# Gamma folded into the first attention's weights, x1 made on GpSimd, fewer steps in a row in the first batch's last norm, and all of y ahead of the first experts

## The chip, the cores and the metric

The kernel runs on one core of one Trainium2 chip. A core has five engines with queues of their own: TensorE (PE; its weight loads are shown apart as PEld), VectorE (DVE), ScalarE (ACT), GpSimd (POOL) and SyncE (SP, which here only issues DMAs). The metric is the device time of one execution in microseconds; lower is better. Each queue is worked off in order, and an instruction at its head that waits for another engine holds up all behind it.

## What is computed

The reference, cut to what matters (8 batches of 512 tokens with 128 channels, all float32):

```python
xn  = layernorm(layernorm(x)) * gamma + beta       # inside the attention
qkv = xn @ w_qkv; q, k, v = heads of 4 x 32
q = q * 32 ** -0.5;  k = softmax(k, over the tokens)
context = k^T v per head;  out = (q context) @ w_out + b_out
attn = out + layernorm(x)
x = x + layernorm(attn)
h = layernorm(x)
ffn = sum over 8 experts of (silu(h @ Wg) * (h @ Wu)) @ Wd     # 128 -> 512 -> 128
x = x + layernorm(ffn)
```

The attention is a linear one: for each batch it comes down to one 128 x 128 matrix (context, masked to the four heads, times w_out), by which q is multiplied. The code calls that matrix `m`, the normed input plus the output bias `x1b`, and the attention's output with the residual `y`.

## The kernel before, in words

**Stages.** A batch is held as four tiles of 128 tokens (`NJ` = 4). Batch 0 goes through `opening()`, which is tuned for latency, since nothing else can run yet; the attention of every later batch is spread over the expert steps of the batches before it. The experts of one batch are 32 steps (8 experts by 4 column blocks of 128); one step is a matmul into `g` (L1080), one into `u` (L1081), a Silu on ACT (L1085) and a product on DVE (L1105). For a batch of 512 tokens the second expert matrix is then applied in `down_pairs` (L935).

**Batch 0.** Its first 16 steps are cut by tokens, so that they can begin before all tokens are ready. The list `units` (L868 to L871) has: steps 0 and 1 for tile 0, steps 0 and 1 for tile 1, steps 2 to 15 for tiles 0 and 1 together, steps 0 to 15 for tiles 2 and 3, and then steps 16 to 31 for all four.

**The order** of every queue is the order of the program text (`manual_schedule`): there is no scheduler. Generators (`prepare`, `first_pieces`, `after_m`) are advanced by `next(...)` where their instructions are to stand, and `plan()` gives for each step the calls that are put behind that step's product.

**The opening**, in order of what needs what:

- The statistics of x (`both_stats`, L189): per tile a bn_stats and a bn_aggr on DVE, then `scale(h)` and a power of -1/2 on GpSimd (L212) for the double norm. A layernorm of a layernorm is computed in one go from mean and variance.
- `norm_apply` (L260) makes `xh`; PE transposes it (L429, L363); ACT and DVE bring it out of PSUM while they apply gamma and beta (L430, L436, L443), which gives `xnT`.
- `keys` (L374): PE product, DVE maximum (L379), ACT Exp (L380). `values`, `turn_keys`, `context`, `query` and `masked` follow; L467 and L468 put `m` together from the two halves of the tokens, whose softmax sums were taken apart.
- `first_norm` (L366) makes x1 on DVE and adds the bias on GpSimd (L372). Tiles 0 and 1 are made in the opening, tiles 2 and 3 in the steps of tile 1 (L971).
- `first_pieces` (L675) handles tiles 0 and 1: PE adds x1b (by a product with the identity) and q m into `y` (L684, L687); then come DVE statistics (L696 to L700), the power for `rstd` on GpSimd (L701), a covariance of x and y (L706), from which the variance of the sum x + norm(y) follows without another pass, a second power (L713), the normed input `z` of the experts (L719), its transpose (L725) and the copy to `zT` (L726), for which the first expert matmul waits.
- `after_m` (L752) does the same for tiles 2 and 3, in pieces behind steps 4 to 13 of the unit of tiles 0 and 1 (L977, L978): y on PE (L762, L765) behind step 4, statistics behind 5, covariance behind 6 and 7, GpSimd's part (L785 to L787) behind 8, norm and residual (L789, L790) behind 9, `z` (L792, which is L260 in the profile) behind 11, and its transpose on PE (L794, L269 in the profile) behind 12.
- `prepare` makes, beside the opening, what the later batches need of the weights: `wqT`, `gwv` and the constant part `mb` of m. `keep_warm` (L161) lets PE do products that nobody reads.

**Weights.** SP issues 24 loads of 256 KB for the experts, one after another, while the opening runs. `weight_sums` (L887) and `differences` (L895 to L897) are elementwise work on GpSimd for the later products.

Of the kernel before, what the change touches and what calls it, by code (L numbers as in the profile page):

```python
# [16 lines left out]
def kernel(  # L17
# [45 lines left out]
    P = 128  # L63
# [75 lines left out]
    gwv = const.tile([P, C], F32, name="gwv")  # L139
    mb = const.tile([P, C], F32, name="mb")  # L140

    def prepare():


        t = ps_acc.tile([P, N], F32, tag="accB", name="w_ps")
        nc.tensor.transpose(t[:, :C], w_qkv_sb[:, 0:C], ident)
        nc.scalar.mul(gwv, w_qkv_sb[:, 2 * C : 3 * C], gamma_sb)
        nc.scalar.mul(wqT, t[:, :C], QSCALE)
        yield
        nc.tensor.matmul(t[:, :1], w_qkv_sb[:, 2 * C : 3 * C], beta_sb, start=True, stop=True)  # L150
        bv = const.tile([P, 1], F32, name="bv")
        nc.scalar.copy(bv, t[:, :1])
        bvw = work.tile([P, C], F32, tag="gs", name="bvw")
        nc.scalar.mul(bvw, w_out_sb, bv)
        yield
        nc.tensor.matmul(t[:, :C], heads, bvw, start=True, stop=True)
        yield
        nc.scalar.copy(mb, t[:, :C])
        yield

    def keep_warm(moving, count=1):  # L161

        t = ps_acc.tile([P, N], F32, tag="accA", name="unread")
        for i in range(count):
            nc.tensor.matmul(
                t[:, : moving.shape[1]], moving[:, :P], moving,
                start=(i == 0), stop=(i == count - 1),
            )
# [20 lines left out]
    def both_stats(src):  # L189

        stats = const.tile([P, NJ, 6], F32, name="stats_0")
        mv = [const.tile([P, 2, 2], F32, name=f"mv_0_{h}") for h in range(2)]
        ve = [const.tile([P, 4], F32, name=f"ve_0_{h}") for h in range(2)]
        rstd = [const.tile([P, 4], F32, name=f"rstd_0_{h}") for h in range(2)]

        def one(j):
            nc.vector.bn_stats(stats[:, j, :], src[:, j])  # L200

        def aggregate(j):
            nc.vector.bn_aggr(mv[j // 2][:, j % 2, :], stats[:, j, :])

        def add(h):
            nc.vector.tensor_scalar_add(ve[h][:, :2], mv[h][:, :, 1], EPS)

        def scale(h):
            nc.vector.scalar_tensor_tensor(
                ve[h][:, 2:], ve[h][:, :2], EPS, mv[h][:, :, 1], ALU.mult, ALU.add  # L210
            )
            nc.gpsimd.tensor_tensor(rstd[h][:, 2:], ve[h][:, 2:], mhalf[:, :2], ALU.pow)  # L212

        for call, i in (
            (one, 0), (one, 1), (one, 2), (aggregate, 0), (aggregate, 1), (one, 3), (add, 0),
            (aggregate, 2), (scale, 0), (aggregate, 3), (add, 1), (scale, 1),
        ):
            call(i)
        return [(mv[h], rstd[h][:, :2], rstd[h][:, 2:], ve[h]) for h in range(2)]
# [91 lines left out]
    def opening():  # L311
# [12 lines left out]
        xnT = work.tile([P, N], F32, tag="xnT", name="xnT_0")  # L324
# [29 lines left out]
        weights = prepare()  # L354
        next(weights)
        keep_warm(w_qkv_sb[:, :W])
# [9 lines left out]
        def first_norm(j):  # L366
            h, i = divmod(j, 2)
            nc.vector.tensor_scalar(
                x1[:, j], xt[:, j], s1[h][0][:, i, 0:1], s1[h][1][:, i : i + 1],
                ALU.subtract, ALU.mult,  # L370
            )
            nc.gpsimd.tensor_tensor(x1b[:, j, :], x1[:, j, :], bias_sb, ALU.add)  # L372

        def keys(h):  # L374
            k_ps.append(bank(f"k_ps{h}", "ps" if h else "u"))
            nc.tensor.matmul(
                k_ps[h][:, :W], w_qkv_sb[:, C : 2 * C], xnT[:, COL[h]], start=True, stop=True
            )
            nc.vector.tensor_reduce(kmax[:, h : h + 1], k_ps[h][:, :W], AX.X, ALU.max, negate=True)  # L379
            nc.scalar.activation(  # L380
                ekT[:, COL[h]], k_ps[h][:, :W], AF.Exp, bias=kmax[:, h : h + 1],
                accum_out=ksum[:, h : h + 1],
            )

        def values(h):
            v_ps.append(bank(f"v_ps{h}", "u" if h else "g"))
            for j in H:
                nc.tensor.matmul(
                    v_ps[h][:, j * C : (j + 1) * C],
                    xnT[:, (2 * h + j) * P : (2 * h + j + 1) * P], w_qkv_sb[:, 2 * C : 3 * C],  # L390
                    start=True, stop=True,
                )

        def turn_keys(h):
# [5 lines left out]
            return t[:, :W]  # L400
# [10 lines left out]
        def query(lo, hi, tag, at=0):  # L411
            if not at:
                q_ps.append(bank(f"q_ps{lo}", tag))
            t = q_ps[-1][:, at : at + (hi - lo) * P]
            r = slice(lo * P, hi * P)
            nc.tensor.matmul(t, w_qkv_sb[:, 0:C], xnT[:, r], start=True, stop=True)
            nc.scalar.mul(qT[:, r], t, QSCALE)
# [10 lines left out]
        for j in H:  # L428
            nc.tensor.transpose(t[:, j * P : (j + 1) * P], xh[:, j, :], ident)  # L429
        nc.scalar.activation(  # L430
            xnT[:, COL[0]], t[:, :W], AF.Identity, bias=beta_sb, scale=gamma_sb
        )
        next(weights)
        norm_apply(xh[:, J[1]], xt[:, J[1]], (s1[1][0], s1[1][2]))
        t = [turn(j, "g") for j in (2, 3)]
        nc.scalar.activation(  # L436
            xnT[:, 2 * P : 3 * P], t[0], AF.Identity, bias=beta_sb, scale=gamma_sb
        )
        next(weights)
        for h in H:  # L440
            nc.gpsimd.tensor_tensor(s1[h][1], s1[h][3][:, :2], mhalf[:, :2], ALU.pow)
        first_norm(0)
        nc.vector.tensor_scalar(xnT[:, 3 * P :], t[1], gamma_sb, beta_sb, ALU.mult, ALU.add)  # L443
        keys(0)
        keys(1)
        values(0)
        values(1)
        t0, t1 = turn_keys(0), turn_keys(1)
        nc.vector.tensor_tensor(kmax[:, 2:3], kmax[:, 0:1], kmax[:, 1:2], ALU.min)

        nc.scalar.activation(part, kmax[:, :2], AF.Exp, bias=kmax[:, 2:3], scale=-1.0)
        for h in H:
            nc.vector.tensor_copy(v[:, COL[h]], v_ps[h][:, :W])
        nc.vector.tensor_copy(ek[:, COL[0]], t0)
        nc.scalar.copy(ek[:, COL[1]], t1)
        query(0, 1, "u")
        context(0)
        context(1)
        query(1, 2, "g")
        nc.vector.tensor_tensor(ksum[:, 2:4], ksum[:, 0:2], part, ALU.mult)  # L460
        nc.vector.tensor_tensor(ksum[:, 2:3], ksum[:, 2:3], ksum[:, 3:4], ALU.add)
        first_norm(1)
        nc.vector.reciprocal(rsum, ksum[:, 2:3])
        masked(0)
        nc.vector.tensor_scalar(part, part, rsum, None, ALU.mult)
        masked(1)
        nc.vector.tensor_scalar(m, m_ps[0][:, :C], part[:, 0:1], None, ALU.mult)  # L467
        nc.vector.scalar_tensor_tensor(m, m_ps[1][:, :C], part[:, 1:2], m, ALU.mult, ALU.add)  # L468
# [4 lines left out]
        keep_warm(flat(xt[:, J[0]]), 2)  # L473
        next(first)
        keep_warm(yn[:, 0], 2)
        next(first)
        rest.extend((first, second, first_norm))
# [197 lines left out]
    def first_pieces(xt, s1, qT, m, x1b, x2, yn, z, zT):  # L675

        mvx, vex = s1[0][0], s1[0][3]
# [3 lines left out]
            for p, t in ((ps, "ps"), (ps_acc, "accB"))  # L681
# [11 lines left out]
        stats, mv, ve, rstd = tile_("pst", 6), tile_("pmv", 2), tile_("pve"), tile_("prs")  # L693
        cov, rv, t, rstd2 = tile_("pco"), tile_("prv"), tile_("pt"), tile_("prt")
        for j in R:
            nc.vector.bn_stats(stats[j], y[j])  # L696
        for j in R:
            nc.vector.bn_aggr(mv[j], stats[j])
        for j in R:
            nc.vector.tensor_scalar_add(ve[j], mv[j][:, 1:2], EPS)  # L700
            nc.gpsimd.tensor_tensor(rstd[j], ve[j], mhalf[:, :1], ALU.pow)  # L701

        nm = const.tile([P, 1], F32, name="pnm_0")

        def covariance(j):
# [3 lines left out]
            nc.scalar.mul(cov[j], cov[j], 2.0 / C)  # L709
# [5 lines left out]
        def residual(j):  # L715
            nc.vector.tensor_tensor(x2[:, j], yn[:, j], xt[:, j], ALU.add)

        def last(j):
            nc.vector.tensor_scalar(  # L719
                z[:, j], x2[:, j], mvx[:, j, 0:1], rstd2[j], ALU.subtract, ALU.mult  # L720
            )

        def turn(j):
            t_ps = ps.tile([P, N], F32, tag="ps", name=f"z_ps_0{j}")
            nc.tensor.transpose(t_ps[:, :P], z[:, j], ident)  # L725
            (nc.vector.tensor_copy if j else nc.scalar.copy)(  # L726
                zT[:, j], t_ps[:, :P].rearrange("c (a i) -> c a i", a=NQ)
            )

        for j in R:  # L730
            nc.vector.reciprocal(rv[j], ve[j])
            nc.scalar.activation(
                rv[j], rv[j], AF.Identity, bias=vex[:, j : j + 1], scale=mv[j][:, 1:2]
            )
        covariance(0)
        nc.vector.tensor_scalar(yn[:, 0], y[0], mv[0][:, 0:1], rstd[0], ALU.subtract, ALU.mult)
        scale(0)
        covariance(1)
        nc.vector.scalar_tensor_tensor(nm, mv[1][:, 0:1], -1.0, rstd[1], ALU.mult, ALU.mult)
        nc.scalar.activation(yn[:, 1], y[1], AF.Identity, bias=nm, scale=rstd[1])  # L740
        residual(0)
        scale(1)
        yield
        last(0)
        turn(0)
        residual(1)
        last(1)
        yield
        turn(1)
        yield  # L750
# [192 lines left out]
    def plan(b, lo, hi, begin):  # L943
# [24 lines left out]
        if hi - lo == 1:  # L968
            if lo:
                for i in range(2):  # L970
                    at(i, lambda i=i: rest[2](2 + i))  # L971
            else:
                p["first"] = lambda: next(rest[0])
        elif b == 0 and begin < FIRST:
            if not lo:
                go = lambda: next(rest[1], None)
                at(4, go, go)  # L977
                for i in (5, 6, 7, 8, 9, 11, 12, 13):  # L978
# [178 lines left out]
```

## Time and profile before

| quantity | value |
|---|---|
| median of 3 runs | 687.84 us (687.75 to 688.28) |
| the profiled execution | 687.67 us |
| its span in the trace | 685.7 us |
| granted TensorE clock, mean | 0.999 |
| PE busy | 678.5 us, 99% of the span |
| DVE, ACT, POOL busy | 301.6, 248.5, 428.2 us |
| share of PE in the chain that ended last | 98% |
| first expert matmul starts at | 17.33 us |
| second half's transpose (L269) starts at | 30.20 us |

The span is the time from the first to the last recorded instruction; the profiled execution is 2.0 us longer than it. The chain that ended last is found from the last instruction backwards, at each step to what released it. A timeline row gives the start, the duration, the engine, the line and the operation with its tiles, and in brackets how long the engine had been idle and what ended that.

### The profile page before, as it was taken

The numbers are of one execution on the slowest core, as the hardware profiler recorded it, in microseconds if no ns is written. First come the engines' busy times: TensorE is split into PE (matmuls) and PEld (weight loads), VectorE is DVE, ScalarE is ACT, GpSimd is POOL, SyncE is SP. The second block draws the span as 40 slices with busy tenths as digits, with TensorE's granted clock in tenths as the row PEclk, the third lists the DMA queues.
The fourth block names the chain that finished last, engine by engine and source line by source line (L and its number), as shares of the span: only waits on it lengthen the run. The fifth ranks groups of instructions, "written<-read, shape, count | busy, mean of one in ns | idle before, by whom it ended". The sixth has DMA issues, their size and how long they took to land.

```text
span 685.7 us, 9319 instructions
## 1 busy us (share of the span) xinstructions
PE 678.5 (99%) x3187; PEld 376.8 (55%) x3187; DVE 301.6 (44%) x806; ACT 248.5 (36%) x486; POOL 428.2 (62%) x535
## 2 busy tenths in 40 slices
PE   8999999999999999999999999999999999999997
PEld 6875565445654455544654446544465445644576
DVE  6656404555055541554324642356513545043425
ACT  5464422454125451254413443145412442033212
POOL 4399895584747656475755749557494583767501
PEclk9999999999999999999999999999999999999999
DMA  8511022010020210101111101100012000010020
GB/s 264 170 32 48 15 61 78 0 61 30 20 77 1 61 32 32 62 21 41 32 46 48 32 31 33 67 26 32 31 33 77 1 31 1 17 62 0 1 78 16
DMA packets 36671, 30.82 MB, mean 45 GB/s; under 512 B 3984, under 2 KB 28048, under 8 KB 36624
## 3 DMA queue, kind: packets, MB, share of 16 engines
q1 hardware_dynamic: 36336, 30.03, 13.7%
q8 instruction: 25, 0.41, 0.3%
q14 instruction: 22, 0.18, 0.1%
q10 hardware_dynamic: 288, 0.20, 0.1%
HBM read 18.42 MB, written 11.80 MB: 44 GB/s over the span
## 4 chain that ended last, share of the span: by engine, by line
PE 98%; DVE 1%; DMA 0%; POOL 0%; issue 0%; ACT 0%; POOLq 0%; DVEq 0%
PE g L1080 32%; PE u L1081 32%; PE accA L935 16%; PE accB L935 12%; PE g_ps L483 1%; PE y_ps L579 1%; PE k_ps L547 1%; PE end L822 1%; DMA x<-in_L_attn_x_dram 0%; PE end_A L822 0%; PE end_B L822 0%; PE c_ps L492 0%; PE wa_ps L504 0%; PE m_ps L498 0%; PE c_ps L406 0%
## 5 line engine op out<-in xcount | busy, mean ns | idle before, releaser
L1105 DVE TENSOR_TENSOR h<-sg,u 128x512 f32<-128x512 f32 (+2 forms) x266 | 172.5, 650 | 336.2 <-PE u L1081 311.3
L1085 ACT ACTIVATE sg<-g 128x512 f32<-128x512 f32 (+2 forms) x282 | 156.4, 556 | 362.4 <-PE g L1080 341.0
L1080 PE MATMUL g<-zT,wg 128*128 128x512 f32 (+2 forms) x564 | 267.0, 555 | 0.4 <-ACT zT L726 0.4
L1081 PE MATMUL u<-zT,wu 128*128 128x512 f32 (+2 forms) x564 | 265.8, 553 | 0.0
L895 POOL TENSOR_TENSOR t<-h 128x512 f32<-128x512 f32 x124 | 157.9, 1274 | 123.4 <-PE accB L935 62.9
L1081 PEld LDWEIGHTS u<-zT,wu 128*128 128x128 f32 x564 | 106.9, 190 | 113.3 <-issue 109.3
L1080 PEld LDWEIGHTS g<-zT,wg 128*128 128x128 f32 x564 | 102.3, 190 | 96.1 <-issue 92.0
L935 PE MATMUL accA<-h,wd 128*64 128x256 f32 x620 | 145.7, 380 | 0.0
L935 PE MATMUL accB<-t,ws 128*64 128x256 f32 x496 | 137.8, 380 | 0.0
L935 PEld LDWEIGHTS accA<-h,wd 128*64 128x64 f32 x620 | 84.3, 137 | 40.7 <-PE u L1081 3.8
L897 POOL TENSOR_TENSOR h<-h,t 128x256 f32<-128x256 f32 x124 | 90.6, 730 | 9.7
L896 POOL TENSOR_TENSOR t<-h,t 128x256 f32<-128x256 f32 x124 | 90.2, 727 | 9.7
L935 PE MATMUL accA<-t,ws 128*64 128x256 f32 x248 | 73.8, 379 | 0.0
L935 PE MATMUL accB<-h,ws 128*64 128x256 f32 x248 | 73.8, 379 | 0.0
L245 POOL TENSOR_TENSOR rstd<-ve,mhalf 128x4 f32<-128x4 f32 (+1 forms) x28 | 32.8, 1170 | 60.3 <-DVE nm L243 49.1
L935 PEld LDWEIGHTS accB<-t,ws 128*64 128x64 f32 x496 | 67.3, 137 | 0.0
L935 PEld LDWEIGHTS accB<-h,ws 128*64 128x64 f32 x248 | 34.0, 137 | 17.9
L935 PE MATMUL accB<-h,wd 128*64 128x256 f32 x124 | 36.9, 379 | 0.0
L935 PEld LDWEIGHTS accA<-t,ws 128*64 128x64 f32 x248 | 34.0, 137 | 0.0
L253 ACT ACTIVATE fn<-q,nm,rstd 128x128 f32<-128x128 f32 x28 | 11.5, 482 | 39.2 <-POOL nm L246 39.2
L253 ACT ACTIVATE x<-x,nm,rstd 128x128 f32<-128x128 f32 x56 | 22.9, 482 | 3.1 <-POOL nm L246 2.4
L186 POOL TENSOR_TENSOR rstd<-ve,mhalf 128x2 f32<-128x2 f32 (+1 forms) x4 | 2.5, 632 | 31.3 <-DVE ve L184 31.2
(202 smaller groups left out, 403.8 us busy)
## 6 DMA issues: line engine op xcount, KB each, us to landing
wg<-in_L_ffn_Wg_dram SPq DMA_DIRECT2D x8, 256.0 KB, 6.0
wu<-in_L_ffn_Wu_dram SPq DMA_DIRECT2D x8, 256.0 KB, 5.9
wd<-in_L_ffn_Wd_dram SPq DMA_DIRECT2D x8, 256.0 KB, 6.1
bounce<-f_blkA SPq DMA_DIRECT2D x8, 256.0 KB, 2.0
fA<-bounce SPq DMA_DIRECT2D x32, 64.0 KB, 2.0
bounce<-f_blkB SPq DMA_DIRECT2D x8, 256.0 KB, 2.1
fB<-bounce SPq DMA_DIRECT2D x32, 64.0 KB, 2.0
x<-in_L_attn_x_dram SPq DMA_DIRECT2D x7, 256.0 KB, 2.7
```

The source lines that it names most:

```text
L245: nc.gpsimd.tensor_tensor(rstd, ve, mhalf[:, :n], ALU.pow)
L253: nc.scalar.activation(d, t, AF.Identity, bias=nm[:, i : i + 1], scale=rstd[:, i : i + 1])
L483: nc.tensor.matmul(g_ps[:, :C], xh[:, j, :], ek[:, :, j * Q : (j + 1) * Q], start=(j == 0), stop=(j == NJ - 1),)
L547: nc.tensor.matmul(k_ps, w_qkv_sb[:, C : 2 * C], self.xnT, start=True, stop=True)
L895: nc.gpsimd.tensor_tensor(t[:, 0:2], h[:, 1::2], h[:, 0:2], ALU.subtract)
L896: nc.gpsimd.tensor_tensor(t[:, 2], h[:, 3], t[:, 0], ALU.subtract)
L897: nc.gpsimd.tensor_tensor(h[:, 1], h[:, 2], t[:, 2], ALU.subtract)
L935: nc.tensor.matmul(o, w, r, start=start, stop=stop)
L1080: nc.tensor.matmul(g_ps[:, :cols], wg_sb[e][:, w], zT, start=True, stop=True)
L1081: nc.tensor.matmul(u_ps[:, :cols], wu_sb[e][:, w], zT, start=True, stop=True)
L1085: nc.scalar.activation(sg[:, :cols], g_ps[:, :cols], AF.Silu)
L1105: nc.vector.tensor_tensor(flat(h2)[:, first : first + cols], sg[:, :cols], u_ps[:, :cols], ALU.mult)
```

## The change

Five things are changed, all in the work of batch 0 up to its first 16 steps.

1. **Gamma goes into the weights.** `prepare` multiplies the key and value weights by gamma on ACT (`gwk`, `gwv`), DVE does the query weights (`gwq`). What comes out of the transposes is only copied (`xhT`). Beta drops out of the keys (a softmax over tokens does not see a constant), enters the queries as a bias `bq`, and the values through `mb`, which is added when `m` is made. `prepare` thus has two products with beta in place of one, and its later pieces stand further back.
2. **GpSimd makes x1** of all four tiles in the opening, with a tensor_scalar in place of DVE's; the bias addition stays there.
3. **The last norm of tiles 0 and 1 has fewer steps in a row.** The scaling of the covariance is folded into constants, `x2` is first left without its means, the mean that belongs to it is one [P, 1] value, and GpSimd puts x2 right later, in place.
4. **All of y precedes the first experts**: the two first pieces of `after_m` are called in the opening, and its other pieces move ahead by one or two steps; the transpose from step 12 to step 11.
5. Order: the statistics of tiles 0 and 1 are aggregated before those of tile 2 begin; both maxima precede the Exps; copies stand in `values` and `turn_keys`, the second ones on ACT; all queries stand behind the contexts; the unread products are fewer and go to another PSUM buffer.

The diff, cut to its core:

```diff
-    def prepare():
+    def prepare(s1):
         t = ps_acc.tile([P, N], F32, tag="accB", name="w_ps")
-        nc.tensor.transpose(t[:, :C], w_qkv_sb[:, 0:C], ident)
+        nc.tensor.transpose(t[:, C : 2 * C], w_qkv_sb[:, 0:C], ident)
+        nc.scalar.mul(gwk, w_qkv_sb[:, C : 2 * C], gamma_sb)
         nc.scalar.mul(gwv, w_qkv_sb[:, 2 * C : 3 * C], gamma_sb)
-        nc.scalar.mul(wqT, t[:, :C], QSCALE)
-        yield
-        nc.tensor.matmul(t[:, :1], w_qkv_sb[:, 2 * C : 3 * C], beta_sb, start=True, stop=True)
-        bv = const.tile([P, 1], F32, name="bv")
-        nc.scalar.copy(bv, t[:, :1])
+        yield
+        for k, i in enumerate((2, 0)):
+            nc.tensor.matmul(
+                t[:, k : k + 1], w_qkv_sb[:, i * C : (i + 1) * C], beta_sb, start=True, stop=True
+            )
+        b = const.tile([P, 2], F32, name="b_vq")
+        nc.scalar.copy(b, t[:, :2])
+        yield
...
         nc.scalar.copy(mb, t[:, :C])
+        nc.scalar.mul(wqT, t[:, C : 2 * C], QSCALE)
+        nc.scalar.mul(bq, b[:, 1:2], QSCALE)
         yield
...
         def scale(h):
-            nc.vector.scalar_tensor_tensor(
-                ve[h][:, 2:], ve[h][:, :2], EPS, mv[h][:, :, 1], ALU.mult, ALU.add
+            nc.vector.tensor_scalar(
+                ve[h][:, 2:], mv[h][:, :, 1], 1 + EPS, EPS * EPS, ALU.mult, ALU.add
             )
             nc.gpsimd.tensor_tensor(rstd[h][:, 2:], ve[h][:, 2:], mhalf[:, :2], ALU.pow)
 
         for call, i in (
-            (one, 0), (one, 1), (one, 2), (aggregate, 0), (aggregate, 1), (one, 3), (add, 0),
-            (aggregate, 2), (scale, 0), (aggregate, 3), (add, 1), (scale, 1),
+            (one, 0), (one, 1), (aggregate, 0), (aggregate, 1), (one, 2), (scale, 0), (one, 3),
+            (aggregate, 2), (aggregate, 3), (add, 0), (scale, 1), (add, 1),
         ):
...
         def first_norm(j):
-            nc.vector.tensor_scalar(
+            nc.gpsimd.tensor_scalar(
                 x1[:, j], xt[:, j], s1[h][0][:, i, 0:1], s1[h][1][:, i : i + 1],
                 ALU.subtract, ALU.mult,
             )
             nc.gpsimd.tensor_tensor(x1b[:, j, :], x1[:, j, :], bias_sb, ALU.add)
...
-        nc.scalar.activation(
-            xnT[:, COL[0]], t[:, :W], AF.Identity, bias=beta_sb, scale=gamma_sb
-        )
-        next(weights)
+        nc.scalar.copy(xhT[:, COL[0]], t[:, :W])
         norm_apply(xh[:, J[1]], xt[:, J[1]], (s1[1][0], s1[1][2]))
         t = [turn(j, "g") for j in (2, 3)]
-        nc.scalar.activation(
-            xnT[:, 2 * P : 3 * P], t[0], AF.Identity, bias=beta_sb, scale=gamma_sb
-        )
-        next(weights)
+        nc.scalar.copy(xhT[:, 2 * P : 3 * P], t[0])
         for h in H:
             nc.gpsimd.tensor_tensor(s1[h][1], s1[h][3][:, :2], mhalf[:, :2], ALU.pow)
-        first_norm(0)
-        nc.vector.tensor_scalar(xnT[:, 3 * P :], t[1], gamma_sb, beta_sb, ALU.mult, ALU.add)
+        for j in range(NJ):
+            first_norm(j)
+        nc.vector.tensor_scalar(gwq, w_qkv_sb[:, 0:C], gamma_sb, None, ALU.mult)
+        nc.vector.tensor_copy(xhT[:, 3 * P :], t[1])
+        nc.vector.tensor_scalar(vx, s1[0][3][:, :2], 1.0, C / 2, ALU.add, ALU.mult)
+        next(weights)
         keys(0)
         keys(1)
+        softmax(0)
+        softmax(1)
         values(0)
         values(1)
-        t0, t1 = turn_keys(0), turn_keys(1)
         nc.vector.tensor_tensor(kmax[:, 2:3], kmax[:, 0:1], kmax[:, 1:2], ALU.min)
+        turn_keys(0)
+        turn_keys(1)
         nc.scalar.activation(part, kmax[:, :2], AF.Exp, bias=kmax[:, 2:3], scale=-1.0)
-        for h in H:
-            nc.vector.tensor_copy(v[:, COL[h]], v_ps[h][:, :W])
-        nc.vector.tensor_copy(ek[:, COL[0]], t0)
-        nc.scalar.copy(ek[:, COL[1]], t1)
-        query(0, 1, "u")
+        next(weights)
         context(0)
         context(1)
+        next(weights)
+        query(0, 1, "u")
         query(1, 2, "g")
+        masked(0)
         nc.vector.tensor_tensor(ksum[:, 2:4], ksum[:, 0:2], part, ALU.mult)
         nc.vector.tensor_tensor(ksum[:, 2:3], ksum[:, 2:3], ksum[:, 3:4], ALU.add)
-        first_norm(1)
         nc.vector.reciprocal(rsum, ksum[:, 2:3])
-        masked(0)
+        masked(1)
         nc.vector.tensor_scalar(part, part, rsum, None, ALU.mult)
-        masked(1)
...
         next(first)
         query(2, 4, "u")
-        keep_warm(flat(xt[:, J[0]]), 2)
+        next(second)
         next(first)
-        keep_warm(yn[:, 0], 2)
+        next(second)
+        keep_warm(flat(xt[:, J[0]]), 1)
         next(first)
...
+        def residual(j):
+            nc.vector.scalar_tensor_tensor(
+                x2[:, j], y[j], rstd[j], xt[:, j], ALU.mult, ALU.add
+            )
+            nc.vector.scalar_tensor_tensor(
+                mean[j], mv[j][:, 0:1], rstd[j], mvx[:, j, 0:1], ALU.mult, ALU.add
+            )
+        def last(j):
+            nc.vector.tensor_scalar(
+                z[:, j], x2[:, j], mean[j], rstd2[j], ALU.subtract, ALU.mult
+            )
...
+        inverse(0)
         covariance(0)
-        nc.vector.tensor_scalar(yn[:, 0], y[0], mv[0][:, 0:1], rstd[0], ALU.subtract, ALU.mult)
+        inverse(1)
         scale(0)
+        residual(0)
         covariance(1)
-        nc.vector.scalar_tensor_tensor(nm, mv[1][:, 0:1], -1.0, rstd[1], ALU.mult, ALU.mult)
-        nc.scalar.activation(yn[:, 1], y[1], AF.Identity, bias=nm, scale=rstd[1])
-        residual(0)
-        scale(1)
         yield
         last(0)
         turn(0)
+        scale(1)
         residual(1)
         last(1)
         yield
         turn(1)
+        for j in R:
+            nc.gpsimd.tensor_scalar(
+                x2[:, j], x2[:, j], mean[j], mvx[:, j, 0:1], ALU.subtract, ALU.add
+            )
         yield
...
                 go = lambda: next(rest[1], None)
-                at(4, go, go)
-                for i in (5, 6, 7, 8, 9, 11, 12, 13):
+                for i in (3, 4, 5, 6, 7, 9, 11):
                     at(i, go)
```

In the new order ACT makes both `zT` copies (with a factor) ahead of the first Silu, and GpSimd's queue has: two powers, two powers, four pairs of tensor_scalar and addition for x1, the two powers of `rstd`, the two last powers, the two corrections of x2, then the second half's work and the weight sums.

## The prediction

> **What bounds the kernel.** I read the page's busy times and its chain first. PE is busy 99% of the span, and the chain that ended last is 98% PE:
>
> ```profile
> PE 678.5 (99%) x3187; PEld 376.8 (55%) x3187; DVE 301.6 (44%) x806; ACT 248.5 (36%) x486; POOL 428.2 (62%) x535
> ...
> PE 98%; DVE 1%; DMA 0%; POOL 0%; issue 0%; ACT 0%; POOLq 0%; DVEq 0%
> ```
>
> From 31 us on, PE's groups show 0.0 us idle. So whatever is won or lost before that moves the end by the same amount, and only three places can change: the start of the experts, products that PE does not have to fit in between them, and PE's waits among the first steps. The chain in order of time shows all three:
>
> ```profile
> 13.03 0.47 PE y_ps_ps L687 x2
> ...
> 14.40 0.57 POOL prs L701
> ...
> 15.65 0.56 POOL prt L713
> ...
> 17.33 0.49 PE g L1080 x2
> ...
> 22.29 0.44 PE y_ps L762 x4
> 22.73 0.45 PE y_ps L765 x4
> ...
> 29.75 0.85 DVE z L260 x2
> 30.60 0.04 issue
> 30.65 0.33 PE z_ps L269
> ```
>
> Up to 17.33 us the path is one latency after another over DVE, ACT, GpSimd and PE. At 22.29 the second half's y takes 0.44 + 0.45 us out of the experts' stream. At 29.75 PE waits for the second half's z.
>
> **Products moved (a sure gain).** y of tiles 2 and 3 goes from behind step 4 into the opening: 0.44 + 0.45 = 0.89 us less in PE's stream. In the opening it stands behind the queries. There PE only does unread products (13.99 to 15.02 and 15.55 to 16.2 us in the timeline) and idles. It needs qT of tiles 2 and 3 (ready at 14.57 before) and x1b of these tiles from GpSimd, below. If the cover is gone, PE stands at y while z waits behind it. Gain **0.89**, at worst 0.
>
> **The wait at 30 us.** PE's last product into u starts at 29.49 and its two passes take 0.43, so the next could start at 29.92; two transposes at 0.11 each make 30.14 for the next g, which starts at 30.82: 0.68 lost. DVE has z of step 11 ready 1.27 us after that step's h begins (29.33 to 30.60); PE asks one step (0.86) earlier than it can have it. After the change z stands behind step 9 and the transpose behind step 11, so there is one more step of 0.86 us. What GpSimd must do before z also moves ahead by two steps. Gain **0.68**, at least 0.5 if z is slowed twice by port waits (below).
>
> **Start of the opening.** The first power on GpSimd starts at 4.87, behind three bn_stats, four small operations and scale. With the aggregates drawn ahead and scale no longer waiting for add, scale ends near 4.36 (start 3.44, two bn_stats 0.40, two aggregates 0.33, one bn_stats 0.20), and the power starts at 4.45 to 4.55. PE takes some back: one more pair of passes for beta (0.2) and the unread product ahead of the transpose (0.2) keep it until about 5.95, so the transposed first half is out at 6.39 instead of 6.61. The copy takes 0.37 (L455, 128x256 out of PSUM) instead of 0.56 (L430): keys(0) at 6.84 instead of 7.26. For tile 3 the gain is 0.41 from the power, 0.12 from copy against tensor_scalar (0.29, L726, against 0.41, L443) and what DVE's first_norm(0) held: ready at 7.19 instead of 7.87. keys(1) can follow keys(0) after its two passes, 7.27 instead of 8.01 (it was released at 7.97 by the copy of mb, which now stands late). **0.74 won** so far. The weights' gamma products on ACT (0.40 each, L147) run from 4.96 to 5.76, beside GpSimd's powers, needed at 6.84; uncovered they would cost 0.40.
>
> **GpSimd makes x1.** No row has a tensor_scalar with two [P, 1] operands on GpSimd. Below: 0.29 us (the affine_select of the identity, one input of 128x128). Above: 0.91, twice the addition, if it made two passes. I take 0.45, the row of the addition on the same tile, engine and kind of access:
>
> ```profile
> L372 POOL TENSOR_TENSOR x<-x,bias_sb 128x128 f32<-128x128 f32 x2 | 0.9, 454 | 3.0 <-DVE rsum L463 3.0
> ```
>
> The four powers end near 7.2 (4.5 + 1.39 + 1.35); four pairs of 0.45 + 0.45, with some 0.1 of gaps each, end at 11.2. The first user of tiles 2 and 3 is at about 13. Queued behind x1 are the powers of rstd, which are due at about 14; so the move costs nothing itself up to 1.1 us for one tensor_scalar (7.2 + 4 x (1.1 + 0.55) = 13.8).
>
> **What it costs DVE.** Here the trace speaks against the change. Small DVE operations that follow a GpSimd operation on whole tiles take as long as it:
>
> ```profile
> 56.89 0.74 DVE L236 TENSOR_SCALAR ve<-mv 128x4 f32<-128x4 f32 x1
> 57.66 1.18 DVE L238 SCALAR_TENSOR_TENSOR ve<-ve,mv 128x4 f32<-128x4 f32 x1
> ```
>
> Their medians are 0.170 and 0.164 us; GpSimd's rows beside them run 56.88 to 57.61 and 57.56 to 58.82. Each waited for one whole operation, one after the other. Products with an operand in PSUM (L1105, 0.42) do not stretch beside GpSimd, and the xh of 5.62 to 6.89 (0.342 each) did not beside the powers. So between 7.2 and 11.2 four operations are exposed, each by 0 to 0.45: vx ahead of the maxima, the minimum (L449 before), and the two ksum operations, now between masked(0) and masked(1). I take half of one for vx and for the minimum and for each of the last two about an eighth, since they come as x1 ends: 0.15 for the path at the maxima, 0.25 at ksum.
>
> The Trainium skill, "SBUF — State Buffer", section "Who interferes with whom", states the same as an exclusive lock: a DVE operation with two SBUF inputs, or a tensor_scalar in a two-port mode, and a GpSimd operation block each other for a whole instruction, the first one wins. By it every one of the four would wait wherever GpSimd is ahead, and the sum below would come out 0.5 us smaller; this trace's rows agree where both streams are dense.
>
> **From the Exps to m.** Exp of the second half: 9.18 becomes 8.63 (keys(1) 0.74 earlier, less 0.15, and less 0.04 because DVE's two maxima now touch). Copy of the second ek: 1.09 later as before (9.18 to 10.27), so 9.72 to 10.09; the copy of v on ACT (0.37) lies before it and ends at 9.6. PE had 0.34 of query in front of the contexts, now 0.22 of mb's product, earlier. The contexts end at 10.74 instead of 11.58. masked(1) now stands behind the ksum chain, which needs part (ACT, 10.38): three operations at about 0.18 from 10.5, so 10.95 undisturbed, 11.20 with the port. From masked(1) to y was 13.03 - 11.62 = 1.41: y at **12.61**, won **0.42**. Bounds: 0.67 without any port wait, -0.5 with a full one at each place. ACT's three small operations for mb, wqT and the bias (0.26, 0.26, 0.19) and two queries (0.28 to 0.46) end before 11.7, the table load of 1.28 before 13.1; the second queries come at 13.4, so they stay hidden.
>
> **From y to g.** 17.33 - 13.03 = 4.30 before. The residual and ACT's scaling leave the path between the two powers: prt began 1.25 after prs and now only waits for the second prs (two take 1.08 of GpSimd): 0.16 won. g at 17.33 - 0.42 - 0.16 = 16.75.
>
> **A new wait behind it.** GpSimd's queue has the correction of x2 of tile 0 right behind tile 1's last power, with nothing to wait for. So it starts as that power ends, and tile 1's z, released by the same power, meets it. The rows of z at 29.67 (0.389 and 0.616 against 0.342) show such a meeting. z is then 0.45 late; 0.22 of that is slack (PE has the first two products to do), so tile 1's steps start **0.23** later. Bounds: 0 and 0.69 (tensor_scalar of 0.91).
>
> **Sum.** 0.42 + 0.16 - 0.23 + 0.89 + 0.68 = 1.92. The profiled execution took 687.67, so 685.75. The median of the runs is 0.17 above it: **685.9 us**. 0.2% is 1.38 us, about what a measurement of this kernel can tell from no change.
>
> **Rivals.**
>
> - *No port waits* (18%): DVE falls between GpSimd's operations, or a tensor_scalar takes 0.29. 0.67 + 0.16 + 0.89 + 0.68 = 2.40: 685.4. For it: most DVE work there reads PSUM.
> - *GpSimd is the slow engine* (15%): 0.91 for one tensor_scalar. x1 ends at 13.0, each ksum operation waits up to 0.9, y comes at 13.5 (-0.5), tile 1 loses 0.69. -0.5 + 0.16 - 0.69 + 1.57 = 0.54: 687.3. For it: even two elements take 0.7 in a power.
> - *Slower* (8%): a tensor_scalar above 1.1 us. Then x1 holds the powers of rstd, and each 0.1 above that costs 0.4 there and 0.1 at x2. The gain is gone at about 1.1 to 1.3; at 2.0 x1 ends at 17.4, 3.4 after 14, and the sum is 0.58 - 3.4 - 1.8 + 1.57 = -3.0: 690.8. Against it: the addition with two inputs takes only 0.454.
> - *The clock drops* (3%): there are fewer unread products. PE's warm-up passes take 0.43 us until about 4.9, twice the 0.215 of later ones; some 2 us of this would cost 1 us: 686.9. Against it: y of tiles 2 and 3 fills the place, and the longest gap stays below 1 us (0.54 before).
> - *The change does nothing at all* can't be: 0.89 us leave PE's stream.
>
> **Chances and range.** The forecast 56%, with 685.3 to 686.5. Faster by over 0.2% (below 686.46): most of the forecast and all of the first rival, 0.73; within: 0.18; slower: 0.09. The range 685.0 to 687.4 takes in the first rival (with 0.3 for the error of my steps) and the slow engine.
>
> **What would show it.** L372's new companion at 0.29 to 0.91; the first power at 4.5; y at 12.6; the first g at 16.75; no y between the experts' steps; no wait for DVE at the second half's transpose; tile 1's z beginning with GpSimd's correction beside it. Wrong if GpSimd's x1 runs past 14 us, or if PE's passes return to 0.43 after 16 us.

## The result, and the profile after

The time after is 686.28 us (median of 18 runs, 685.7 to 687.11) against 687.92 us before (18 runs, 687.16 to 688.66): ratio 0.9974, 95% [0.9968, 0.9981]. So 1.64 us are won where 1.94 were forecast (687.84 to 685.9); the interval, 0.19% to 0.32% faster, leaves out no change and takes in the 0.2% that the forecast took for about what a measurement of this kernel can tell. The profiled execution took 686.39 us with a span of 684.3; before it was 687.67 and 685.7.

Busy times and the chain by engine, on the page of the changed kernel:

```profile
PE 677.5 (99%) x3183; PEld 377.1 (55%) x3183; DVE 300.0 (44%) x802; ACT 247.8 (36%) x487; POOL 433.0 (63%) x541
...
PE 98%; DVE 0%; POOL 0%; issue 0%; ACT 0%; POOLq 0%; DVEq 0%
```

PE still bounds the kernel. DVE's share of the chain now rounds to 0% (1% before), and GpSimd (POOL) is 4.8 us busier. The chain in order of time (start, length, what) says more:

```profile
0.76 5.46 PE unread L176 x12
6.22 0.21 PE w_ps L151
6.43 0.51 PE w_ps L156 x4
6.94 0.29 PE xh_ps L438 x2
...
7.67 1.13 PE k_ps L387 x4
...
13.36 0.47 PE y_ps_accA L697 x2
...
17.48 0.49 PE g L1095 x2
...
28.12 0.43 PE u L1096 x2
28.55 0.22 PE z_ps L280 x2
28.77 0.43 PE g L1095 x2
```

The right half of the forecast is at the bottom: the second half's two transposes stand between u and g without a gap, no DVE step is in the chain there, and no y product is left between the experts' steps. The wrong half is at the top. Up to 7.2 us the chain is PE itself: the unread products (twelve instructions, the last two on w_qkv), the weight transpose, the two products with beta (four instructions), and only then the first transposes of the input. y comes at 13.36 instead of 12.61, the first g at 17.48 instead of 16.75 (before: 17.33).

The timeline of the same kernel (start, length, engine, line, operation; in brackets the idle time before it and what ended it):

```profile
4.56 1.40 POOL L223 TENSOR_TENSOR rstd<-ve,mhalf 128x2 f32<-128x2 f32 x2 [2.44 <-DVE ve L220]
5.16 1.06 PE L176 MATMUL unread<-w_qkv_sb 128*128 128x256 f32 x2
6.80 0.42 PE L438 MATMUL xh_ps<-ident,xh 128*128 128x128 f32 x2
7.34 0.79 POOL L379 TENSOR_SCALAR x<-x,mv,rstd 128x128 f32<-128x128 f32 x1
9.53 0.45 POOL L383 TENSOR_TENSOR x<-x,bias_sb 128x128 f32<-128x128 f32 x1
9.63 0.37 DVE L457 TENSOR_TENSOR kmax<-kmax 128x1 f32<-128x1 f32 x1
17.48 1.58 POOL L766 TENSOR_SCALAR x<-x,pme,mv 128x128 f32<-128x128 f32 x2
17.52 0.48 DVE L732 TENSOR_SCALAR z<-x,pme,prt 128x128 f32<-128x128 f32 x1 [0.28 <-POOL prt L720]
```

GpSimd's first power is where it was forecast (4.56). The half it serves is not transposed until 6.80. GpSimd's new operation takes 0.79 us, not 0.45. Two DVE operations beside GpSimd's work are stretched. The minimum takes 0.37 and ends at 10.00, just after an addition of the bias (to 9.98); tile 1's z takes 0.48 (tile 0's: 0.34) inside the correction of x2. In the kernel before, the product on w_qkv and the minimum stood so:

```profile
5.13 0.70 PE L165 MATMUL unread<-w_qkv_sb 128*128 128x256 f32 x2
9.18 0.16 DVE L449 TENSOR_TENSOR kmax<-kmax 128x1 f32<-128x1 f32 x1
```

### The profile page after: what moved, and what is told of

Its sections match the earlier page's. It is cut to its first block, busy times and chain, and to the rows that moved or that the text cites. A ratio compares the mean times of both kernels' runs of the same rounds, so it can differ in the third digit from the quotient of the medians.

```text
span 684.3 us, 9310 instructions
## 1 busy us (share of the span) xinstructions
PE 677.5 (99%) x3183; PEld 377.1 (55%) x3183; DVE 300.0 (44%) x802; ACT 247.8 (36%) x487; POOL 433.0 (63%) x541
## 4 chain that ended last, share of the span: by engine, by line
PE 98%; DVE 0%; POOL 0%; issue 0%; ACT 0%; POOLq 0%; DVEq 0%
PE g L1095 32%; PE u L1096 32%; PE accA L954 16%; PE accB L954 12%; PE g_ps L493 1%; PE y_ps L589 1%; PE k_ps L557 1%; PE unread L176 1%; PE end L841 1%; PE end_A L841 0%; PE end_B L841 0%; PE wa_ps L514 0%; PE m_ps L508 0%; PE c_ps L502 0%; PE k_ps L387 0%; POOL prs L750 0%
```

## The experiments

Two theories stood after the first profile of the change. **A**: the gain is y and the wait at 30 us alone; the opening's gain is held up by PE's unread product and small products ahead of the first transposes, which run at half clock (what is meant by that is said below, under "When the clock comes up"). **B**: GpSimd's x1 and the waits it puts on DVE eat the opening's gain. The kernel before took 688.06 (20 runs) beside the first four kernels, 688.27 (15 runs) beside the next three.

**y alone.** The kernel before, with y of tiles 2 and 3 in the opening and the following pieces one or two steps earlier:

```diff
+        first_norm(2)
+        first_norm(3)
         next(first)
...
-        keep_warm(flat(xt[:, J[0]]), 2)
+        next(second)
+        next(second)
...
-                at(4, go, go)
-                for i in (5, 6, 7, 8, 9, 11, 12, 13):
+                for i in (3, 4, 5, 6, 7, 9, 11):
```

(The products go to other PSUM buffers, so that they need not wait.)

> One part alone: the kernel before, with y of tiles 2 and 3 ahead of the first experts (their x1 made by VectorE right after m) and the later pieces ahead by one or two steps, as in the change; all else of the opening as before. Theory A (the opening won nothing because TensorE reached the first transpose late; the measured gain is that of y and of the wait at 30 us): 0.89 + 0.68 = 1.57 us less than before, so about 686.4, as fast as the whole change. Theory B (GpSimd's x1 and the port took the opening's gain): the same 686.4. Theory C (the opening wins 0.3 to 0.4 in most executions, and the profiled one was an unlucky one): also 1.57 less, but then the whole change must be faster than this by 0.3 or more. The first g starts at 17.3 to 17.4 in its profile.

Measured: 686.35 us (8 runs), ratio 0.9974 [0.9964, 0.9984], the same as the whole change. Its chain where the wait was:

```profile
28.43 0.43 PE u L1081 x2
28.86 0.22 PE z_ps L269 x2
29.08 0.43 PE g L1080 x2
```

PE goes from u through the transposes to g without a gap. 1.71 us are won, where the two terms of the forecast give 0.89 + 0.68 = 1.57.

**The change without y.**

```diff
         query(2, 4, "u")
-        next(second)
         next(first)
-        next(second)
...
-                for i in (3, 4, 5, 6, 7, 9, 11):
+                at(4, go, go)
+                for i in (5, 6, 7, 8, 9, 11, 12):
```

> One part undone: the change without the move of y (y of tiles 2 and 3 behind step 4 again, pieces behind steps 5 to 9, 11 and 12). Theory A: nothing is left of the gain, 687.9 within 0.3. Theory B: the same, or slower by up to 0.3. Theory C: 0.3 to 0.4 faster than before, 687.5. The profile must show y between the steps (0.89) and the wait of about 0.7 before the second half's transpose again.

Measured: 688.19 us (11 runs), ratio 1.0003 [0.9994, 1.0012]. In its chain y and the wait are back:

```profile
22.73 0.45 PE y_ps L779 x4
23.17 0.45 PE y_ps L782 x4
...
29.77 0.42 DVE h L1119
30.20 0.86 DVE z L271 x2
31.09 0.33 PE z_ps L280
```

Everything else that the change does comes to nothing that the median shows.

**The change without the unread product on the weights.**

```diff
         weights = prepare(s1)
-        keep_warm(w_qkv_sb[:, :W])
         next(weights)
```

> The change without the unread product on w_qkv, which stands ahead of the weight transpose, the products with beta and the first transposes of x. Theory A: TensorE reaches the first transpose of x 0.43 us earlier with the clock up, and up to 0.86 at half clock; the first g starts 0.4 to 0.8 earlier than in the change, 685.5 to 685.9. Theory B: the path is GpSimd's and VectorE's, so no change (686.3). If the clock came up later for want of the product, the passes of the first transposes would last 0.43 instead of 0.3 and nothing would be won.

Measured: 685.61 us (5 runs, 685.49 to 685.82), ratio 0.9963 [0.9951, 0.9976]: 0.67 below the change's median and 0.44 below the kernel of the next experiment, which ran beside it and is as fast as the change. Its chain:

```profile
0.76 4.60 PE unread L176 x10
5.36 0.21 PE w_ps L151
5.58 0.75 PE w_ps L156 x4
6.32 0.29 PE xh_ps L437 x2
...
17.04 0.49 PE g L1094 x2
```

The transposes come 0.62 earlier than in the change's profile, though the four beta products now take 0.75 (they wait for beta's transfer too), and the first g 0.44 earlier; x was there at the same time in both (3.42 and 3.45). This is theory A's case.

**x1's subtraction back on DVE** (the additions stay on GpSimd; tile 0 at its old place, tile 1 behind masked(1), tiles 2 and 3 behind m):

```diff
-            nc.gpsimd.tensor_scalar(
+            nc.vector.tensor_scalar(
                 x1[:, j], xt[:, j], s1[h][0][:, i, 0:1], s1[h][1][:, i : i + 1],
```

> The change with the tensor_scalar of x1 on VectorE again (tile 0 after the second half of xh, tile 1 behind masked(1), tiles 2 and 3 after m), GpSimd only adds the bias. Theory A: no change against the whole change, 686.3 within 0.2, since 0.79 us tensor_scalars on GpSimd were hidden. Theory B: y and the first g come 0.3 to 0.7 earlier, 685.6 to 686.0. In the profile the minimum of the maxima is 0.16 instead of 0.37.

Measured: 686.05 us (7 runs), ratio 0.997 [0.9959, 0.9981]. That lies between the two expectations, 686.1 to 686.5 and 685.6 to 686.0. The minimum is back at its old length:

```profile
9.35 0.15 DVE L456 TENSOR_TENSOR kmax<-kmax 128x1 f32<-128x1 f32 x1
```

So GpSimd did stretch it, but y comes at 13.33 and the first g at 17.45, as in the change, although the first transposes come 0.28 earlier (6.52). DVE's own subtraction for tile 1 (0.34) now stands ahead of m. So this exchange of engines gains nothing that the profile shows; that the waits cost nothing isn't shown by it, since it takes them away and puts an operation on the path in their place.

**The change again, and without both.** The first of the next two is the change unaltered; the second takes out the unread product and puts x1's subtraction on DVE (the last two edits together).

> The whole change, unaltered, beside the next two on the same chip. Theory A: about 686.3. Its profile is another sample of the moment at which TensorE's clock comes up: if that is near 4.6 us, as in the profile of before, the passes of the unread products end near 5.7 instead of 6.2 and the first g starts near 17.0; if it is near 6.2 again, at 17.5.

> The change without the unread product on w_qkv and with x1's tensor_scalar on VectorE. Theory A: with TensorE's queue free the next limits are VectorE's xh and the Exps, GpSimd's x1 is still covered: 685.5 within 0.3, like the change without the unread product (685.61). Theory B': once TensorE is free, port waits show: 685.0 to 685.3.

Measured: 686.12 (5 runs, 685.86 to 686.24) for the change, 685.63 (5 runs, 685.58 to 685.71; ratio 0.9962 [0.9948, 0.9975]) without both. The two ranges don't touch, 0.49 lies between the medians, and that is what the unread product's removal gave alone (685.61): moving x1's subtraction from GpSimd to DVE adds nothing to it.

**The kernel before without its unread product on the weights.**

```diff
         next(weights)
-        keep_warm(w_qkv_sb[:, :W])
         next(weights)
```

> The kernel before without its unread product on w_qkv. Theory A in its general form (two half-clock passes, 0.86 us, in front of the first transposes hold the path in most executions, in either kernel): 0.2 to 0.5 faster than before, 687.5 to 687.8; less than in the change, because here the power comes later (4.87) and a product for mb stands ahead of the second half's transposes. If the product cost something only in the changed order: no difference from before (688.0 within 0.2).

Measured: 687.86 us (11 runs), ratio 1.0 [0.9991, 1.0009]. A general form of theory A, by which the product costs wherever it stands, expected 0.2 to 0.5 and missed. The chain shows why:

```profile
5.62 0.29 ACT wqT L148
5.95 0.40 PE w_ps L150 x2
6.37 0.17 ACT bv L152
6.57 0.41 ACT bvw L154
7.11 0.46 PE w_ps L156 x2
7.57 0.12 PE xh_ps L362
```

In the old order a chain over ACT (wqT, bv, bvw) stands in front of the second half's transposes at 7.57, so a shorter queue on PE buys little: y alone, which has the old order with the product and ran at half clock as long, has that transpose at 7.74 and the first g at 17.86, against 17.70 here. The change takes that chain away, and PE's queue is what comes next.

**When the clock comes up.** By half clock is meant the length of PE's passes: the two instructions of the w_qkv product hold PE for 0.86 in the profile of after and for 0.43 in the early one below. The clock itself isn't seen to rise: the profile's granted clock reads 1.00 from 0.7 to 7.0 us in every profile, so its moment is read from the passes alone. The change's opening and the old one could not be compared at equal passes yet: the w_qkv product took 0.70 in the profile of before and 1.06 in that of after. So five more profiles were taken, two of the kernel before and three of the change, both unaltered:

> The kernel before, unaltered, for a second profile of it. If the profile shown before was one in which TensorE's clock came up early (its unread products end at half the pitch after 4.6 us) and most executions are not, then here the clock comes up near 6.2, the products with beta end near 6.5 instead of 6.0, and the first g starts at 17.7 to 17.9 instead of 17.33: the forecast was summed against a better opening than the usual one. If the clock has nothing to do with it, the first g starts at 17.3 again.

> The same once more, since the moment of the clock differs between executions: a first g near 17.3 with an early clock, 17.7 to 17.9 with a late one.

> The whole change, unaltered, one look: for the moment at which TensorE's clock comes up and the first g at that moment. So far this kernel came up at 6.65 and 6.26 us with the first g at 17.48 and 17.35. Theory (the half clock stretches what stands ahead of the first transposes): a profile in which the clock comes up near 4.5 us shows the w_qkv product at about 0.45 instead of 0.86, the first transposes at 6.0 to 6.2 instead of 6.75 to 6.94, the first g at 16.7 to 16.9 and a time near 685.6. Rival (the queue's length alone, whatever the clock): the first g stays at 17.2 or later with an early clock. If the clock comes up late again (after 6 us): first g 17.3 to 17.5, 686.1 to 686.4, and nothing is told apart.

> The same kernel, second look, with the same two cases: early clock, first g at 16.7 to 16.9 (theory) or at 17.2 or later (rival); late clock, 17.3 to 17.5.

> The same kernel, third look, with the same two cases: early clock, first g at 16.7 to 16.9 (theory) or at 17.2 or later (rival); late clock, 17.3 to 17.5. Three late ones out of three would be a hint that the moment hangs on the kernel's order, since the three looks at the kernel before all came up early.

Both new profiles of the kernel before came up early, so its expected late case was not seen. The change came up early in its 3rd profile (the first of the three), late in the 4th and in between in the 5th. The early one, in the timeline:

```profile
4.82 0.59 PE L176 MATMUL unread<-w_qkv_sb 128*128 128x256 f32 x2
5.73 0.53 PE L438 MATMUL xh_ps<-ident,xh 128*128 128x128 f32 x2
...
8.62 0.80 POOL L379 TENSOR_SCALAR x<-x,mv,rstd 128x128 f32<-128x128 f32 x1
8.96 0.15 DVE L457 TENSOR_TENSOR kmax<-kmax 128x1 f32<-128x1 f32 x1
...
10.81 0.46 POOL L383 TENSOR_TENSOR x<-x,bias_sb 128x128 f32<-128x128 f32 x1
10.91 0.38 DVE L470 TENSOR_TENSOR ksum<-ksum 128x1 f32<-128x1 f32 x1
```

All profiles together, each from its own execution (the unread product on w_qkv and the transposes from the timelines, where the modelled end of the last pass makes the product 0.2 longer than it holds PE; y and g from the chains; "x there at" is the start of the first statistics, which wait for x; the last column is the execution's time less the first g):

| kernel | x there at | w_qkv product, us | first transposes at | y at | first g at | time | after first g |
|---|---|---|---|---|---|---|---|
| before | 3.44 | 0.70 | 6.02 | 13.03 | 17.33 | 687.67 | 670.34 |
| before, 2nd profile | 3.15 | 0.70 | 5.75 | 12.95 | 17.24 | 687.47 | 670.23 |
| before, 3rd profile | 3.16 | 0.70 | 5.74 | 12.89 | 17.19 | 687.39 | 670.20 |
| before without the product | 3.12 | none | 6.20 | 13.40 | 17.70 | 687.86 | 670.16 |
| change without y | 3.27 | 1.06 | 6.69 | 13.58 | 17.71 | 688.19 | 670.48 |
| y alone | 3.51 | 1.01 | 6.37 | 13.57 | 17.86 | 686.50 | 668.64 |
| change | 3.45 | 1.06 | 6.80 | 13.36 | 17.48 | 686.39 | 668.91 |
| change, 4th profile, late | 3.38 | 1.06 | 6.69 | 13.30 | 17.43 | 686.41 | 668.98 |
| change again, 2nd profile | 3.50 | 1.06 | 6.61 | 13.23 | 17.35 | 686.12 | 668.77 |
| change, 5th profile, in between | 3.58 | 0.78 | 6.25 | 13.04 | 17.17 | 685.87 | 668.70 |
| change, 3rd profile, early | 3.41 | 0.59 | 5.73 | 12.89 | 17.02 | 685.84 | 668.82 |
| x1 on DVE | 3.13 | 1.05 | 6.52 | 13.33 | 17.45 | 686.17 | 668.72 |
| without the product | 3.42 | none | 6.19 | 12.90 | 17.04 | 685.82 | 668.78 |
| without both | 3.15 | none | 5.49 | 12.71 | 16.82 | 685.63 | 668.81 |

Two things are read from it. The last column falls into two groups: 670.28 on the mean of the five profiles that keep y among the experts, 668.79 on the mean of the nine that don't. That is 1.49 us. Nothing else in the change moves it by more than 0.3, by which profiles of one kernel differ (668.70 to 668.98 for the change). And among the five profiles of the unaltered change the first g follows the first transposes: from 6.80 down to 6.25 the transposes give 0.55 and g 0.31, and from there to 5.73 another 0.52 and 0.15. PE's queue is the same in all five, and x was there at 3.38 to 3.58, latest in the 5th profile, so its arrival isn't what orders them. The moment at which the passes shorten is therefore a cause, and not the queue's length alone; the queue rival (17.2 or later even with an early clock) falls at 17.02. The last 0.52 of the transposes gives only 0.15 because the early profile's chain no longer runs through PE's queue: it goes from x's transfer over the statistics and GpSimd's powers to the second half's transposes (6.44). The theory's own 16.7 to 16.9 was not reached either.

## Why the prediction was right, and where it failed

**Products moved, and the wait at 30 us: right.** 0.89 + 0.68, less the 0.07 that tile 1 really lost, make 1.50; the table shows 1.49. y alone brings the median of the whole change, and the change without y brings none of it.

**Start of the opening: failed.** The step put as "keep it until about 5.95" is the one. It priced the added products at full clock, 0.2 for beta and 0.2 for the unread product. In the profile of after they ran at half clock: the unread product holds PE for 0.86 (the chain's 5.46 less the 4.60 of the first ten), the beta products for 0.51, and the first transposes begin at 6.80. They are 0.85 late (6.80 against 5.95), and y is 0.75 late. In the early profile, where the transposes come at 5.73 and so no later than forecast, y is at 12.89: 0.47 of the 0.75 goes with the late clock, and the other 0.28 is the next point. The trace of before had the warning. Its first products at the fast pitch come at about 4.9, which the forecast named under the rival of the clock, but only for what a drop would cost; it didn't ask what the opening costs if the clock comes up later than in this one execution.

**0.42 at y: too much even with the early clock.** In the early profile of the change keys(0) come at 6.83 (forecast 6.84), but y at 12.89 instead of 12.61. keys(1) start at 7.47 instead of 7.27; ksum, which the forecast let start at 10.5, stands behind masked(0) until 10.72, and its second operation waits out GpSimd's addition (0.38 for 0.16 undisturbed; it ends at 11.29, the addition at 11.27). Against the kernel before at a like clock (12.89 to 13.03) 0 to 0.14 is won, not 0.42; 0.14 is against the profile in which x was there at a like moment (3.44, here 3.41).

**From y to g: right in size.** 4.30 before; 4.12 after (13.36 to 17.48), 4.13 in the early profile. 0.16 forecast, 0.17 to 0.18 measured.

**The opening's balance.** At an early clock the first g is at 17.02 against 17.19 to 17.33, 0.17 to 0.31 won; the 0.31 is against the profile in which x came at a like moment, in the other two it was there 0.26 earlier. At a late clock the change's 17.35 to 17.48 stand against 17.70 (before without the product) and 17.86 (y alone), 0.2 to 0.5 won; but the change without y, which has the same opening, stands at 17.71. So the opening wins some tenths of the 0.58 forecast in most of these pairs, and next to nothing in one (17.71 against 17.70). The medians don't resolve them: change 686.28 against y alone 686.35, change without y 688.19 against before 688.06, with intervals of 0.4 to 0.7 us to each side. In the two profiles first shown the opening even seems to lose 0.15, because before was caught with an early clock and after with a late one.

**GpSimd makes x1: size wrong, cost right.** 0.792 for one tensor_scalar, near the upper bound of 0.91 and not the 0.45 taken; x1 ends at 12.6 instead of 11.2, and before the powers of rstd. That is why it costs nothing there. The row of the two-input addition was the wrong neighbour. The Trainium skill, "GPSIMD Engine Reference", section "4.1 Engine selection", calls GpSimd about half as fast as DVE with two inputs and roughly at line rate with one; by the rows here the one-input tensor_scalar with two per-partition operands is the slower one, 0.792 against 0.456 for the addition on the same tile.

**What it costs DVE: right in kind, but it is the addition that holds, and it is on the path in some executions.** The forecast exposed four small operations to all of GpSimd's x1. In the profiles of the new opening a small DVE operation that begins during an addition of the bias, with more than its own length of it left, ends 0.01 to 0.02 us after that addition: seven times in six profiles, among them the minimum of 0.37. Beside the new tensor_scalar alone most keep their 0.15 to 0.17 (the early profile's minimum, above, took 0.15), a few take up to 0.29. That is less than the forecast's lock on whole instructions, by which every one of them would wait wherever GpSimd is ahead. So which operation waits, and for how long, hangs on where the two streams happen to meet. In the profile of after, the minimum's wait lies beside the Exps and isn't in the chain. In the change without y two waits are in the chain:

```profile
11.13 0.79 POOL L379 TENSOR_SCALAR x<-x,mv,rstd 128x128 f32<-128x128 f32 x1
11.29 0.29 DVE L469 TENSOR_TENSOR ksum<-ksum,part 128x2 f32<-128x2 f32 x1
12.00 0.46 POOL L383 TENSOR_TENSOR x<-x,bias_sb 128x128 f32<-128x128 f32 x1
12.08 0.40 DVE L473 TENSOR_SCALAR part<-part,rsum 128x2 f32<-128x2 f32 x1
```

The change's 4th profile has the same first transposes (6.69), 0.15 and 0.22 in these places, and y at 13.30 instead of 13.58. So theory B, that GpSimd's x1 takes from the opening's gain, holds in part: 0.28 at y in that execution, near the 0.25 that the forecast had for ksum, and that with a late clock. Without x1's subtraction on GpSimd and without the product the first g comes at 16.82, 0.20 before the change's early profile; but x was there 0.26 earlier in it, so this pair says nothing of the port.

**A new wait behind it: right in kind, a third of the size.** z was 0.14 late instead of 0.45: it ran from 17.52 to 18.00, inside the first of the two corrections (0.796 on the mean, from 17.48), and was stretched, not held to its end. Tile 1's g follows tile 0's after 1.27 us (18.75 - 17.48), 1.20 before. 0.07 lost instead of 0.23.

**The rivals.** None came as priced: GpSimd was slow, but short of the point from which it decides, and the forecast's time held because the failed step (0.58 expected, some tenths come) was only a third of the sum.

**Open.** What part of all executions has the late clock in either kernel isn't known; only profiled ones show it. The first ten unread instructions are the same in all 14 profiles: they take 4.20 to 4.30 in four (all three of the kernel before, and the early one of the change), 4.42 in one and 4.60 to 4.61 in nine. Whether the moment hangs on the kernel too isn't settled by so few. The medians fit both having a mix (the three profiles of before, all early, took 687.39 to 687.67, below its medians of 687.84 to 688.27), but that is argued, not shown.

A better version than both came out of it: the change without the unread product on the weights, 685.61 us, 0.9963 [0.9951, 0.9976] of before.

## What to carry to other kernels

Where one engine is 99% busy, work and waits taken out of its stream come back one for one; here the two such terms came out to within a tenth of a microsecond. The gain from shortening a latency chain ahead of it is only as long as the next queue lets it be. Before you price a step that is freed, list what stands ahead of it in the queue of the engine that does it, warm-up products included, and price that list at the clock it will see. Subtract the time at a common mark (here the first g) from each profile's time: it splits a result of a few tenths into parts that medians can't resolve. Before two single profiles of an opening are set against each other, see whether the input arrived and the passes shortened at like moments in both.

## What the runs showed of the hardware

- The moment at which TensorE's passes halve differs between executions of one kernel; that this is its clock is inferred from the factor of two, since the granted clock reads 1.00 throughout. In the five profiles of the unaltered change the two instructions of the w_qkv product, which start 4.1 to 4.4 us after the first warm-up product, took 0.59, 0.78 and three times 1.06 us. The Trainium skill, "TensorE: Matmul & The Clock Gate", section "Part 1: The HAM clock gate (the "warmup" mystery)", has it that the activity window runs freely and doesn't reset when a kernel starts, so that the number of slow products varies from run to run; the spread here agrees.
- A tensor_scalar on GpSimd (128x128, one tensor and two per-partition operands) takes 0.792 us, and 0.796 for the correction of x2; the two-input addition takes 0.456.
- A DVE operation on one element per partition takes 0.15 us alone. Where it begins during GpSimd's two-input addition on a whole tile, with more than 0.15 of it left, it ends 0.01 to 0.02 us after it, and took 0.32 to 0.41 (the minimum, the second ksum operation); beside GpSimd's tensor_scalar the minimum took 0.15 in three profiles. Whether it meets an addition changes from execution to execution of one kernel (the minimum took 0.37 in the profile of after and 0.15 in the early one).
- The moment at which the kernel's first input is there differs as well: the first statistics start between 3.12 and 3.58 us in the 14 profiles, and between 3.38 and 3.58 in the five of the unaltered change.
